# Attention output and its sums regrouped by transfers between partitions instead of by transposes

## The chip, the cores and the metric

The kernel runs on one core of one Trainium2 chip. The core has five engines with a queue of instructions each: TensorE (PE, matmuls and transposes, results in PSUM), VectorE (DVE), ScalarE (ACT), GpSimd (POOL, which does not read PSUM here) and SyncE (SP), which here does nothing but issue DMAs. The metric is device time in microseconds. Before the change two runs took 737.3 and 737.54 us, median 737.42.

## The reference

One PixArt block: batch 16, 256 tokens, width 256, 16 heads of 16, with a condition vector, a self attention, a cross attention to 256 context tokens and an MLP.

```
x_norm = ln(x) * (1 + scale_a) + shift_a
q, k, v = split(x_norm @ W_qkv + b_qkv)                 # 16 heads of 16
attn = softmax(q @ k.T / 4) @ v                         # per head
x = x + gate_a * (attn @ W_proj + b_proj)
q_c = ln(x) @ W_qc + b_qc;  k_c, v_c = split(ln(context) @ W_kvc + b_kvc)
x = x + softmax(q_c @ k_c.T / 4) @ v_c @ W_cproj + b_cproj
h = gelu((ln(x) * (1 + scale_m) + shift_m) @ W_mlp1 + b_mlp1)
x = x + gate_m * (h @ W_mlp2 + b_mlp2)
```

Everything is float32. Products are made of float32r parts: each operand is split into a high part and a low part (what is left), and three products are summed.

## The kernel before

**Units.** Each of the 16 self attentions ("s") and 16 cross attentions ("c") is a unit; the list `seq` (line 786) starts with five s units and then alternates. The loop at line 1219 runs over the units, and each unit has eight steps (`beat`, line 1120). Step k of unit n works on several units at once: it makes the transposed scores and exponentials of two head pairs of unit n (`t_part`, `exp`), the plain scores of unit n+1 and their maxima (`s_tile`; one TensorE product into a bank, one VectorE reduce out of it; two banks, `s0` and `s1`), parts of the Q, K and V projections of later units, and the end of earlier units. After the eight steps of the last unit, the MLP of all samples follows, two matmul stages in four chunks each; its first chunks are interleaved with the end of the last unit in a hand-written order, the string `BE` in `E_` (line 55), whose words are looked up in `done` (line 1232).

**Two lanes.** TensorE's array is used in two halves of 64 rows. `PLAN` (line 1108) gives for every step four strings: words issued before, lane x (rows 0 to 63), lane y (rows 64 to 127), and words issued after. `beside` (line 476) merges the two lanes' instructions by their lengths into TensorE's one queue. "s" and "t" are the scores, a letter with a number is so many matmuls of a projection ("Q12"), "T" and "U" are transposes of a normalised input, "m0" and "m1" of maxima, "E" is the exponential, "o0" and "o1" are the output products. Each half transpose of a tile (`half_turns`, line 342) is four or one pieces of 64 rows; the second half's first piece waits for the first half's last.

**Attention output.** `av_part` (line 769) multiplies exponentials by values. The values tile `vts` (line 86) has 32 columns per head: 16 values and 16 ones, so each head gives 16 rows of output and 16 equal rows of sums; four heads fill 128 rows. Two of these products (one "o" word) fill a bank, which ScalarE copies to the tile oT: [128 rows = 4 heads x 32, 2 groups, 256 tokens]. Each unit has two such tiles, hf = 0 (from "o0") and hf = 1 (from "o1", in the next unit's step 0).

**From there to the projection**, in `build_post` (line 601):

- `pieces` and `halves` (lines 620, 627): four transposes of 128 x 128 per tile, in halves ("A0" in step 6, "A1" in step 2), into psA. Tokens are now rows.
- `norm` (line 630): VectorE takes the reciprocal of 16 sums per row and multiplies, into the tile A ("n0" after step 7, "n1" after step 3).
- `aT` (line 640, made by `transposed`, line 358): four more transposes ("a", step 5) into psT, a ScalarE copy out of PSUM (`evac`, "ae"), and on GpSimd `cut` (line 381, "ac"), a rounded copy (xTh) and a difference (xTl).
- `proj` or lane words "P": 24 half-array matmuls with the projection's weights, in lane x for the unit before and in lane y for the one before that; then `end` ("pe", ScalarE), `add` (GpSimd) and `store`.

**Order.** TensorE, VectorE, ScalarE, GpSimd and SP all keep the order in which the program is written (the class `InOrder`); an engine whose next instruction waits holds up all that stands behind it in its queue. All DMAs of the loop are issued by SP: per unit four transfers for K's high parts, two for K's low part, the same for Q, two small ones for the maxima, a load, and for every second unit a store and a broadcast of gates. The values of K and Q go to a tile `big` in which each head has its rows.

Of the kernel before, what the change touches and what calls it, by code (L numbers as in the profile page):

```python
# [21 lines left out]
def pixart_block(  # L22
# [8 lines left out]
    B, N, H = x.shape  # L31
    NH = 16
    HD = H // NH
    SCALE = HD ** -0.5
    NT = N // P
    KC = H // P
# [18 lines left out]
    E_ = {'CUT': 8, 'LN': {'s': 'pool', 'c': 'pool', 'q': 'pool'}, 'ON': (1, 1, 1), 'L0': -16, 'L1': 1, 'S0': -7, 'A0': 0, 'T0': 1, 'S1': 5, 'A1': 7, 'L2': 9, 'T1': 9, 'S2': 32, 'AP': 23, 'DV': (0, 1), 'HP': (1, 0), 'BZ': {}, 'AV': {1: [(1, 2), (1, 3)], 9: [(0, 0), (0, 1)]}, 'AHEAD': (0, 0, 0, 0, 0, 2), 'TW': {(21, 6): 'cb', (23, 5): 'u0', (23, 7): 'u1', (25, 2): 'u2', (27, 3): 'u3', (27, 7): 'h2a', (28, 0): 'l2 h0p u5', (28, 2): 'h1p', (28, 4): 'h3p', (28, 7): 'u4 u6', (29, 0): 'l3d', (29, 1): 'l0', (29, 2): 'l1', (29, 7): 'h5p', (30, 1): 'u7 h6d h7p', (30, 3): 'h4p', (31, 1): 'l4 l6d', (31, 2): 'l5d x2', (31, 4): 'l7', (31, 7): 'b2'}, 'BE': 'G0 av P g0 A1 G1 G2 N1 F7 g1 S0 PF s2 G3 aT aL p2 a2 G4 x3 b3 S1 S2 T2 C r0 G5 S3 G6 S4 s3 CF x4 F8 g2 G7 S5 F9 p3 S6 G8 a3 r1 G9 F10 G10 T3 g3 b4 S7 s4 F11 S8 S9 F12 G11 p4 a4 F13 r2 S10 G12 x5', 'XP': 1, 'IL': 1, 'MF': 0, 'SH': 4, 'RAMP': 1, 'HA': 1, 'MP': 16, 'W': (7, 1, 0, 0), 'PRE': 'load z0kp silu b12 turn brow L0a z0qp L0b b4 L0d T0t hik scale lok sc1 lg L1a b5 T0h L1b T0l ld2 one0 shift b3 K0a bk hiq lc L1d lp L2a K0m loq K0h T1t K0y0p T1h K0l K0x0 bq hiv K0l0 T1l z1qp K0x1 K0l1 Q0a Q0m K1a K0y1p lov Q0h Q0l Q0x1 K1b Q0l0 bv z1kp V0a Q0l1 Q0x0 Q1a Q1b L2b Q1y0 K1x0 V0b K1l b9 Q0y0p Q0y1p Q1l', 'SL': {(-1, 0): 'L2c ld3 K1l0 K1y1', (-1, 1): 'Q1l0 T2t Q1y1 V1a T2h Q1x0 K1l1 K1x1 T2p', (-1, 2): 'wm V1b Q1x1 z2kp vone', (-1, 3): 'ga K1y0', (-1, 4): 'pb M0 Q1l1 ld4 gs L3a', (-1, 5): 'L3b L3p one1', (-1, 6): 'one2 K2a L3c K2m', (-1, 7): 'z2qp mods cb', (0, 0): 'gm lx sp0', (0, 2): 'sp1 sc2', (0, 3): 'sp3', (0, 6): 'sp2', (1, 4): 'sp4'}}  # L55
# [35 lines left out]
    ones = const.tile([8, N], F32, name="ones")  # L91
# [16 lines left out]
    brow = const.tile([32, P], F32, name="brow")  # L108
# [151 lines left out]
    wm = []  # L260
# [223 lines left out]
    def to_stack(W, src, bias, dst, which, name):  # L484
# [30 lines left out]
        def low_pool():  # L515
            o.lo = work.tile([P, KC, N], F32R, tag="qkl", name=f"l_{name}", bufs=3)
            y = work.tile([P, KC, N], F32, tag="A", name=f"y_{name}", bufs=1)
# [83 lines left out]
    def build_post(u):  # L601
# [18 lines left out]
        def pieces(hf):  # L620
            o.ps = ps_gen(f"psA{hf}_{name}", SHORT)
            return [u.oT[hf][:, r, t * P:(t + 1) * P] for t in range(NT) for r in range(2)]

        def turn(hf):
            whole(pieces(hf), o)

        def halves(hf):
            return half_turns(pieces(hf), o)

        def norm(hf):  # L630
            if hf == 0:
                o.A = work.tile([P, NT, H], F32, tag="A", name=f"A_{name}", bufs=1)
            pv = o.ps.rearrange("p (x h c) -> p x h c", x=4, h=4)
            rc = work.tile([P, 4, 4, 1], F32, tag="rc", name=f"rc{hf}_{name}")
            DVE.reciprocal(rc, pv[:, :, :, HD:HD + 1])
            A = o.A.rearrange("p t (r f) -> p (t r) f", r=2)[:, :, 64 * hf:64 * hf + 64]
            DVE.tensor_tensor(A.rearrange("p x (h i) -> p x h i", h=4),
                              pv[:, :, :, 0:HD], rc.to_broadcast([P, 4, 4, HD]), ALU.mult)

        aT = transposed(lambda: o.A, f"a{name}", pool=True)  # L640

# [38 lines left out]
        o.aT, o.begin, o.gate, o.turn, o.norm, o.proj, o.end, o.add, o.store = aT, begin, gate, turn, norm, proj, end, add, store  # L680
        u.post, o.halves, o.n = o, halves, u.n
# [368 lines left out]
    word["vone"] = lambda: [POOL.memset(v[:, :, :, HD:], 1.0) for v in vts]  # L1050
# [43 lines left out]
    def visit(n, k, home=sp):  # L1094
# [25 lines left out]
    def beat(n, k):  # L1120
# [8 lines left out]
        whole_p = prev and prev.n == nu - 2  # L1129
# [12 lines left out]
        def attention(v, hf):  # L1142
# [12 lines left out]
            "Vk": on(q2 and hasattr(q2, "V"), lambda: q2.V.keep()),  # L1155
# [3 lines left out]
            "ae": on(p1, lambda: p1.aT.evac()), "ac": on(p1, lambda: p1.aT.cut()),  # L1159
            "n1": on(p1, lambda: p1.norm(1)), "n0": lambda: cur.post.norm(0),  # L1160
# [20 lines left out]
            "A1": on(p1, lambda: p1.halves(1)), "A0": lambda: cur.post.halves(0),  # L1181
            "a": on(p1, lambda: p1.aT.halves()),
# [47 lines left out]
    for b in range(2):  # L1230
# [3 lines left out]
        "A1": lambda: o.turn(1), "N1": lambda: o.norm(1), "aT": o.aT.turn, "aL": lambda: (o.aT.high(), o.aT.low_dve()),  # L1234
# [90 lines left out]
```

## Time and profile before

| | |
|---|---|
| median of two runs | 737.42 us |
| profiled execution | 737.4 us, of it 735.6 us span |
| granted TensorE clock | 0.999 |
| busy: PE, DVE, ACT, POOL | 728.9, 584.8, 555.5, 546.3 us |
| DMA packets, bytes | 94825, 90.60 MB |
| attention loop, two units (295.71 to 327.99 us) | 32.28 us |

The span is the time from the first to the last instruction that the profiler saw. Rows of the profile have the form "line engine operation out<-in", and line 51 stands in all of them, since a helper issues every instruction: operations are told apart by their tiles. s is a plain score, st a transposed score, o the output product, psA and psT_a the transposes of the attention output, ps_k, ps_q, ps_v and ps_P the projections, mx the maxima. A trailing s or c names the kind of unit. A time-ordered view has the start in us, the time taken, then the engine and the instruction; SPq is SP's queue. "64*128 64x256" is a matmul of 64 rows by 128 columns of weights with 64 x 256 data, and a "+1 forms" marks that other shapes are in a group. In a bracket stands the idle time before an instruction and what ended it.

### The profile page before, as it was taken

The page shows a single profiled execution, that of the slowest core. Times are in us where ns is not written, and L with a number is a line of the kernel's source. Part 1 is how long each engine was busy: PE and PEld are TensorE (multiplying, and loading weights), DVE is VectorE, ACT ScalarE, POOL GpSimd, SP SyncE. Part 2 cuts the span into 40 slices and gives each one's busy share as a digit, 9 for nine tenths or more (in the row PEclk, how much of TensorE's full clock was granted, in tenths as well). Part 3 has the DMA queues.
Part 4 walks back from the last instruction along what each step waited for, and adds up shares of the span by engine and source line. Part 5 has one row for each costly group of instructions (what it writes and reads, how often), then busy time and mean ns, then how long its engine had stood idle before and what let it go on. Part 6 is the DMA issues. An engine that isn't in the chain of part 4 may idle for free.

```text
span 735.6 us, 25307 instructions
## 1 busy us (share of the span) xinstructions
PE 728.9 (99%) x10112; PEld 644.8 (88%) x10112; DVE 584.8 (79%) x1217; ACT 555.5 (76%) x959; POOL 546.3 (74%) x571
## 2 busy tenths in 40 slices
PE   9999999999999999999999999999999999999997
PEld 9878888888888888888888888888889999999997
DVE  4788898989888888988888989888735577687772
ACT  3268898888888888888888888899887655555553
POOL 6777688869687786968778798788657766767753
PEclk9999999999999999999999999999999999999999
DMA  6754454543545454454545555455312323323331
GB/s 190 205 166 142 125 142 134 141 122 101 155 114 155 125 144 137 107 152 112 160 126 139 143 156 146 126 151 140 96 60 58 102 61 98 98 90 102 87 77 38
DMA packets 94825, 90.60 MB, mean 123 GB/s; under 512 B 9266, under 2 KB 90452, under 8 KB 94708
## 3 DMA queue, kind: packets, MB, share of 16 engines
q1 hardware_dynamic: 94244, 88.20, 42.8%
q8 instruction: 80, 1.31, 0.8%
q0 software_dynamic: 192, 0.52, 0.3%
q14 instruction: 37, 0.30, 0.1%
q10 hardware_dynamic: 272, 0.26, 0.1%
HBM read 26.97 MB, written 8.46 MB: 48 GB/s over the span
## 4 chain that ended last, share of the span: by engine, by line
PE 93%; DVE 3%; POOL 2%; issue 1%; ACT 1%; DMA 1%; SPq 0%; POOLq 0%; ACTq 0%
PE s L51 18%; PE o L51 16%; PE st L51 16%; PE ph L51 10%; PE ps_q L51 5%; PE ps_qc L51 4%; PE ps_v_c L51 3%; PE ps_kc L51 3%; PE ps_P_s L51 3%; PE ps_k L51 2%; PE ps_v_s L51 2%; PE ps_P_c L51 2%; DVE mx L51 1%; PE psT_q L51 1%; PE ps_h L51 1%; PE psA_s L51 1%
## 5 line engine op out<-in xcount | busy, mean ns | idle before, releaser
L51 DVE TENSOR_REDUCE mx<-s 128x2 f32<-128x512 f32 x504 | 324.8, 684 | 64.4 <-PE s L51 57.7
L51 ACT ACTIVATE pt<-st 128x1024 f32<-128x1024 f32 x252 | 258.9, 1027 | 16.4 <-PE st L51 10.4
L51 PE MATMUL s<-big 63*128 63x256 f32 (+1 forms) x1024 | 184.0, 297 | 0.2
L51 PEld LDWEIGHTS s<-big 63*128 63x128 f32 (+1 forms) x1024 | 133.4, 186 | 18.7 <-DVE l_kc L51 6.6
L51 PE MATMUL st<-big 64*128 64x256 f32 (+1 forms) x1024 | 134.6, 298 | 0.5 <-ACT pt L51 0.2
L51 POOL TENSOR_TENSOR hl<-hf,hh 128x512 fp32r<-128x512 f32 x64 | 87.0, 1361 | 52.9 <-ACT hh L51 52.8
L51 PE MATMUL o<-pt,v 128*32 128x256 f32 x2048 | 123.8, 382 | 0.0
L51 PEld LDWEIGHTS st<-big 64*128 64x128 f32 (+1 forms) x1024 | 96.3, 186 | 16.1 <-issue 13.1
L51 PEld LDWEIGHTS o<-pt,v 128*32 128x32 f32 x2048 | 60.1, 110 | 41.4
L51 ACT ACTIVATE hf<-ph,bT 128x256 f32<-128x256 f32 x114 | 47.8, 471 | 33.1 <-PE ph L51 33.0
L51 ACT ACTIVATE hh<-ph,bT 128x256 fp32r<-128x256 f32 x114 | 47.9, 472 | 28.0 <-PE s L51 14.4
L51 ACT COPY oT<-o 128x512 f32<-128x512 f32 x63 | 36.9, 586 | 33.1 <-PE o L51 33.1
L51 PE MATMUL st<-big,hh 128*128 128x256 f32 x256 | 46.7, 282 | 0.0
L51 PE MATMUL s<-big,hh 128*128 128x256 f32 x256 | 46.7, 281 | 0.0
L51 PE MATMUL ph<-wkch,wself 128*128 128x256 f32 x224 | 44.4, 282 | 0.0
L51 PE MATMUL ph<-wqch,wself 128*128 128x256 f32 x224 | 44.3, 282 | 0.0
L51 PE MATMUL ps_k<-xTh_s,wself 64*128 64x256 f32 (+1 forms) x232 | 43.6, 294 | 0.0
L51 POOL TENSOR_SCALAR xn_c<-c,mv_c,rs_c 128x256 f32<-128x256 f32 x32 | 39.0, 1227 | 1.7
L51 PE MATMUL ps_q<-xTh_s,wself 64*128 64x256 f32 (+1 forms) x240 | 39.7, 282 | 0.0
L51 PE MATMUL ps_P_s<-wself,xTh_as 64*128 64x256 f32 x256 | 39.1, 282 | 0.0
L51 PEld LDWEIGHTS s<-big,hh 128*128 128x128 f32 x256 | 39.0, 189 | 0.0
L51 PEld LDWEIGHTS st<-big,hh 128*128 128x128 f32 x256 | 39.0, 189 | 0.0
(250 smaller groups left out, 2500.4 us busy)
## 6 DMA issues: line engine op xcount, KB each, us to landing
big<-h_kc SPq DMA_DIRECT2D x64, 128.0 KB
big<-h_qc SPq DMA_DIRECT2D x64, 128.0 KB
big<-h_k SPq DMA_DIRECT2D x62, 128.0 KB
big<-h_q SPq DMA_DIRECT2D x62, 128.0 KB
big<-l_k SPq DMA_DIRECT2D x32, 128.0 KB
big<-l_q SPq DMA_DIRECT2D x32, 128.0 KB
g<-gd SPq DMA_DIRECT2D x16, 256.0 KB
c<-in_ctx_dram SPq DMA_DIRECT2D x16, 256.0 KB
```

The source lines that it names most:

```text
L51: i = f(*a, **k)
```

## The change

The transposes and the normalisation with tokens as rows go. The values tile now alternates one value and one column of ones, so row 2i of a head's 32 is output i and every odd row is the sum. Per tile two DMAs (`lift`) gather rows by partition stride: the even rows of oT into the tile N (64 rows of 512, which is the layout that the projection needs), and one row of sums per head into the tile S, cut into pieces of 32 (64 rows of 32). When both halves are there, VectorE inverts S in place, 128 x 32 (`recip`). `put` writes it to DRAM, and `get` reads it back so that each head's 512 inverse sums stand in 16 rows (tile R). GpSimd multiplies N by R (`norm`), and `cut` splits the product as before. The step plan is rewritten: the projection of a unit is now in steps 2 to 6 of the unit two later, in both lanes; V's lane x is one unit earlier; the words "d0", "d1" (lift), "rc", "rw", "rr", "ym" take the places shown. Two small tiles of the first steps share the slot of oT; A's slot has two buffers; the third unit's value projection is done before the loop ("V2a V2b").

```diff
-    ones = const.tile([8, N], F32, name="ones")
+    ones = work.tile([8, N], F32, tag="oT", name="ones")
...
-            ACT.copy(vt[:, :, :, 0:HD], o.ps.rearrange("p (t h i) -> p t h i", t=NT, h=NH))
+            ACT.copy(vt[:, :, :, 0:32:2], o.ps.rearrange("p (t h i) -> p t h i", t=NT, h=NH))
...
-        def norm(hf):
...
+        def lift(hf):
+            if hf == 0:
+                o.N = work.tile([P, 2, N], F32, tag="A", name=f"N_{name}", bufs=2)
+                o.S = work.tile([P, 32], F32, tag="rc", name=f"S_{name}")
+            rows = slice(64 * hf, 64 * hf + 64)
+            SP.dma_start(o.S[rows], u.oT[hf][1:128:32].rearrange("h r (j e) -> h (r j) e", e=32))
+            SP.dma_start(o.N[rows].rearrange("p r n -> p (r n)"), u.oT[hf][0:127:2].rearrange("p r n -> p (r n)"))
+
+        def recip():
+            DVE.reciprocal(o.S, o.S)
+
+        def put():
+            o.rd = dram.tile([P, 32], F32, tag="rd", name=f"rd_{name}", bufs=3)
+            SP.dma_start(o.rd, o.S)
+
+        def get():
+            o.R = work.tile([P, 2, N], F32, tag="y", name=f"R_{name}", bufs=2)
+            SP.dma_start(o.R.rearrange("p r n -> p (r n)"),
+                         o.rd.rearrange("(a j) e -> a (j e)", j=16).unsqueeze(1).to_broadcast([8, 16, 512]))
+
+        def norm(eng=POOL):
+            eng.tensor_tensor(o.N, o.N, o.R, ALU.mult)
+            aT.y = o.N
...
     PLAN = [
-        ("kh", "s t m1", "m1 t s", "m1s kH E o1 add gate kl"),
-        ("c1", "s t Q12", "t P2 s P10", "L1 ld kL E"),
-        ("", "s t T pe A1 V3", "s t Q4 T A1 Q1", "hadd E L2 Te Tc c2"),
-        ("", "s t V9", "Q1 t s Q6", "E n1"),
-        ("qh store", "s t", "s t qH", "E L3 o0 ql qL"),
-        ("", "t s a E m0 K6", "t s V4 a m0 V2", "ae ac m0s e5 lc s1"),
-        ("", "s t K1 A0 K5 U E", "V2 t s V4 U A0", "begin e6 Vk Ue s6"),
-        ("", "s t P12", "K2 t s K1 K9", "E n0 Uc s7 e7"),
+        ("", "s t m1", "kh m1 kH s t", "E o1 m1s add gate kl"),
+        ("c1", "s t Q12", "s t V11 d1 V1", "ld E"),
+        ("kL", "L1 s Vk t T P4", "t Q1 s Q3 T", "L2 rc E Te Tc c2"),
+        ("", "s t P8", "Q1 t s Q7", "E rw"),
+        ("e5 qh store", "s t", "s t", "qH E L3 o0 rr ql qL"),
+        ("s1", "t s K1 U m0 K4 E", "t P5 s U m0", "m0s lc e6 Ue Uc"),
+        ("", "K1 s t K6", "s6 P3 t ym s P4", "begin E"),
+        ("", "s t pe V12", "K3 t s K9", "E d0 s7 hadd e7 ac"),
     ]
...
-        on_x = {"Q": (q2, "Q"), "V": (q2, "V"), "K": (q3, "K"), "P": (None if whole_p else p1, None)}
-        on_y = {"Q": (q2, "Q"), "V": (q2, "V"), "K": (q3, "K"), "P": (p2, None)}
+        on_x = {"Q": (q2, "Q"), "V": (q3, "V"), "K": (q3, "K"), "P": (p2, None)}
+        on_y = {"Q": (q2, "Q"), "V": (q2 if n else None, "V"), "K": (q3, "K"), "P": (p2, None)}
...
-        "A1": lambda: o.turn(1), "N1": lambda: o.norm(1), "aT": o.aT.turn, "aL": lambda: (o.aT.high(), o.aT.low_dve()),
+        "A1": lambda: o.lift(1), "N1": lambda: (o.recip(), o.put()), "aT": o.get, "aL": lambda: (o.norm(), o.aT.cut()),
```

At the end of attention the string `BE` is unchanged: "av P g0 A1 G1 G2 N1 F7 g1 S0 PF s2 G3 aT aL p2 a2 G4 x3 b3 S1 S2 T2 C", where p2 and a2 are the power and the product of an MLP layernorm, T2 its transposes on TensorE, and C the last unit's projection.

More of the change, by code (lines that the diff above doesn't have):

```diff
@@ L106, in load_x @@
         SP.dma_start(X[b], tok(x, b))
-    brow = const.tile([32, P], F32, name="brow")
+    brow = work.tile([32, P], F32, tag="oT", name="brow")
     def stage(w_ap, c0, name, tag="pt", bufs=5, t=None, q=SP):
@@ L516, in low_pool @@
             o.lo = work.tile([P, KC, N], F32R, tag="qkl", name=f"l_{name}", bufs=3)
-            y = work.tile([P, KC, N], F32, tag="A", name=f"y_{name}", bufs=1)
+            y = work.tile([P, KC, N], F32, tag="A", name=f"y_{name}", bufs=2)
             for f in range(KC):
@@ L618, in gate @@
             POOL.tensor_tensor(o.xg, X[b], bc_t(G[b][:, 1]), ALU.add)
[L620 to L628, printed above, removed]
-        def norm(hf):
-            if hf == 0:
[L632 to L640, printed above, removed]
+        def lift(hf):
+            if hf == 0:
+                o.N = work.tile([P, 2, N], F32, tag="A", name=f"N_{name}", bufs=2)
[15 more added lines that the diff above has]
+            aT.y = o.N
+        aT = transposed(None, f"a{name}", pool=True)
         def proj(half):
@@ L679, in build_post @@
         o.W, o.src, o.tok, o.name = W, aT, True, f"P_{name}"
-        o.aT, o.begin, o.gate, o.turn, o.norm, o.proj, o.end, o.add, o.store = aT, begin, gate, turn, norm, proj, end, add, store
-        u.post, o.halves, o.n = o, halves, u.n
+        o.lift, o.recip, o.put, o.get = lift, recip, put, get
+        o.aT, o.begin, o.gate, o.norm, o.proj, o.end, o.add, o.store = aT, begin, gate, norm, proj, end, add, store
+        u.post, o.n = o, u.n
     def heads(g):
@@ L1049, in pixart_block @@
         word[f"sp{i}"] = lambda i=i: f_split(i)
-    word["vone"] = lambda: [POOL.memset(v[:, :, :, HD:], 1.0) for v in vts]
+    word["vone"] = lambda: [POOL.memset(v[:, :, :, 1:32:2], 1.0) for v in vts]
     for n, f in (("load", f_load), ("silu", f_silu), ("turn", f_turn), ("brow", f_brow),
@@ L1128, in beat @@
         p1, p2, p3 = (v and v.post for v in map(unit, (n - 1, n - 2, n - 3)))
-        whole_p = prev and prev.n == nu - 2
         if p2 and p2.n > nu - 3:
@@ L1154, in beat @@
             "qH": on(q2 and hasattr(q2, "Q"), lambda: q2.Q.send_high()), "qL": on(q2 and hasattr(q2, "Q"), lambda: q2.Q.send_low()),
-            "Vk": on(q2 and hasattr(q2, "V"), lambda: q2.V.keep()),
+            "Vk": on(n and q2 and hasattr(q2, "V"), lambda: q2.V.keep()),
             "m1s": lambda: m_send(cur, 1), "m0s": on(nxt, lambda: m_send(nxt, 0)),
```

9 lines of the change are left out of this document (4 added, 5 removed).

## The prediction

> **What bounds the kernel now.** I read the page first: the shares of the engines, then the chain that ended last, then the groups. After that came sums over two attention units in mid-kernel, and the time-ordered views of single engines inside them.
>
> ```profile
> PE 728.9 (99%) x10112; PEld 644.8 (88%) x10112; DVE 584.8 (79%) x1217; ACT 555.5 (76%) x959; POOL 546.3 (74%) x571
> PE 93%; DVE 3%; POOL 2%; issue 1%; ACT 1%; DMA 1%; SPq 0%; POOLq 0%; ACTq 0%
> L51 DVE TENSOR_REDUCE mx<-s 128x2 f32<-128x512 f32 x504 | 324.8, 684 | 64.4 <-PE s L51 57.7
> core 0: us, PE busy (x) PEld busy (x) DVE busy (x) ACT busy (x) POOL busy (x), PEclk, DMA share, GB/s
> 295.71:327.99 32.28, 32.27 (x534) 27.41 (x535) 28.05 (x61) 27.24 (x43) 24.54 (x27) 1.00 0.50 138
> ```
>
> TensorE carries 93% of the chain, and VectorE's largest idle time (57.7 us) is spent waiting for score matmuls. So time goes where TensorE's instruction queue goes. The last row is two units (one self, one cross): 32.28 us, 16.14 a unit, at full granted clock. VectorE (14.0 us a unit) and ScalarE (13.6) are not far behind, so a gain on TensorE is capped: VectorE would stop it 2 us further on.
>
> **What is removed on TensorE.**
>
> ```profile
> L51 PE MATMUL psA_s<-ident,oT 64*128 64x64 f32 x256 | 29.3, 227 | 0.0
> L51 PE MATMUL psA_c<-ident,oT 64*128 64x64 f32 (+1 forms) x252 | 27.3, 226 | 0.0
> L51 PE MATMUL psT_as<-ident,A_s 64*128 64x64 f32 x128 | 13.1, 223 | 0.0
> L51 PE MATMUL psT_ac<-ident,A_c 64*128 64x64 f32 (+1 forms) x124 | 13.0, 225 | 0.0
> 300.25 0.22 PE L51 MATMUL psA_s<-ident,oT 64*128 64x64 f32 x1
> 300.29 0.28 PE L51 MATMUL ps_qc<-xTh_q,wqch 64*128 64x256 f32 x1
> 300.31 0.28 PE L51 MATMUL psA_s<-ident,oT 64*128 64x64 f32 x2
> 300.41 0.28 PE L51 MATMUL ps_qc<-xTh_q,wqcl 64*128 64x256 f32 x1
> 300.44 0.22 PE L51 MATMUL psA_s<-ident,oT 64*128 64x64 f32 x1
> ```
>
> All 760 transposes go: 31 units of 24, and 16 more around the last one. Busy times mislead here, since two halves of the array run at once. The starts tell the price: four transposes begin between 300.25 and 300.44, one every 0.062 us, while the other half starts a matmul every 0.12 us. A unit's 24 cost 24 x 0.062 / 2 = 0.74 us of the two-lane stream, as both lanes of the new plan are again of equal length.
>
> **What is removed and added on VectorE and ScalarE.**
>
> ```profile
> L51 DVE TENSOR_TENSOR A_s<-psA_s,rc_s 128x256 f32<-128x256 f32 x32 | 13.6, 425 | 1.1
> L51 DVE RECIPROCAL rc_s<-psA_s 128x16 f32<-128x16 f32 x32 | 8.0, 248 | 0.0
> 302.76 0.66 PE L51 MATMUL s<-big 63*128 63x256 f32 x4
> 315.60 0.42 PE L51 MATMUL s<-big 63*128 63x256 f32 x4
> ```
>
> Per unit VectorE loses 2 x (0.425 + 0.248) = 1.35 us and gains one reciprocal of 128x32 (about 0.25, the price of 128x16); ScalarE loses the copy of the transposed tile out of PSUM. Neither is the bound, but position counts: both old pairs stood between the score reduces of two steps, and the score banks are single. Behind such a pair four score matmuls take 0.66 us, elsewhere 0.42: 0.24 us lost. One of the two places (step 7 to step 0) becomes empty; I credit 0.16 of its 0.24, since the step also has an output product to hide part. At the other place the new reciprocal stands one step earlier, with a wait (below), and I count it even with the old pair.
>
> **What is added on GpSimd.** One 128x512 product a unit.
>
> ```profile
> L51 POOL TENSOR_TENSOR t_s<-t_s,g 128x512 f32<-128x512 f32 x16 | 20.7, 1293 | 0.0
> 317.94 0.61 POOL L51 CAST xTh_c<-y_c 128x512 fp32r<-128x512 f32 x1 [2.66 <-ACT y_c L51]
> 323.78 0.61 POOL L51 CAST xTh_ac<-y_ac 128x512 fp32r<-128x512 f32 x1 [3.86 <-ACT y_ac L51]
> ```
>
> 1.29 us on an engine that has 12.3 us of work in 16.1: 13.6 in about 15.2. It is hidden as long as the 2.7 and 3.9 us of waiting shown above exist. Behind it in GpSimd's order stand the next layernorm products (2.4 us) and the split of the attention output (1.9). The projection that needs that split now comes two steps into the next unit, one unit later than the product it projects, so there is room of about 1 us. I cost it at nothing; without the cover it would be up to 1.29 us a unit.
>
> **What is added on SP's queue.** Six DMAs a unit: two gathers of sums, two of outputs, one to DRAM, one broadcast back. The trace has no such gather, but it has SP's issue times, here for one whole unit:
>
> ```profile
> 312.43 0.55 SPq L51 DMA_DIRECT2D big<-m  x1
> 313.07 2.97 SPq L51 DMA_DIRECT2D big<-h_k  x4
> 316.09 0.59 SPq L51 DMA_DIRECT2D x<-in_x_dram  x1
> 316.78 1.18 SPq L51 DMA_DIRECT2D big<-l_k  x2
> 318.05 0.54 SPq L51 DMA_DIRECT2D x2d<-t_c  x1
> 319.47 2.48 SPq L51 DMA_DIRECT2D big<-h_q  x4
> 322.05 1.20 SPq L51 DMA_DIRECT2D big<-l_q  x2
> 323.89 0.55 SPq L51 DMA_DIRECT2D big<-m  x1
> 324.49 0.39 SPq L51 DMA_DIRECT2D c<-in_ctx_dram  x1
> 324.94 0.46 SPq L51 DMA_DIRECT2D g<-gd  x1
> ```
>
> Eighteen issues take 10.9 us, 0.61 each. Six more at 0.6 make 14.5 of the 15.2 us that I expect of a unit: 95%, in the heavier of the two kinds of unit (the other has 14 issues now: no loads, no store, no gates). Bounds for one new issue are 0.39 (the loads from DRAM) and 0.74 (a quarter of the key sends); I take 0.6, the row of transfers of the same 128 KB. Followed through the new order, nothing waits long: the query sends, behind the put, leave for the broadcast 2.5 us in which the put can land; the low query part, behind the broadcast, lands some 1 us before the score step that reads it. So SP costs nothing, with hardly anything in hand.
>
> **The new wait.** The reciprocal at the end of step 2 waits for a gather issued in step 1, and behind it on VectorE stand the reduces of step 3, whose banks hold up TensorE's scores. How long a transfer takes to land is read off the four-part transpose in the MLP stage:
>
> ```profile
> 605.11 2.58 SPq L51 DMA_DIRECT2D yT<-z  x4
> 609.37 1.74 DVE L51 TENSOR_SCALAR z<-yT,sc,cpT 128x256 f32<-128x256 f32 x2 [1.50 <-DMA yT<-z]
> 627.12 2.49 SPq L51 DMA_DIRECT2D yT<-z  x4
> 632.37 1.41 DVE L51 TENSOR_SCALAR z<-yT,sc,cpT 128x256 f32<-128x256 f32 x2 [2.02 <-DMA yT<-z]
> ```
>
> The last of four parts is issued 1.9 us after the first; its data serve VectorE 2.3 us later (607.1 to 609.4), in the second case 3.4. The gather can issue about 1.6 us after the output product ends (copy 0.6, then the maxima's row, then SP), and lands 3.9 after it; steps 1 and 2 and their reduces take about 3.7. So VectorE waits 0.2 us, at 3.4 us landing 1.3. The first is what I counted even; the second costs up to 1 us a unit.
>
> A rule speaks against this step. The Trainium skill, "DMA: Bandwidth & Descriptors", section "Why a DMA increments its semaphore by 16 and not by 1", says that a DMA spreads over the largest number of engines, up to 16, that divides the slowest dimension of both sides. No row of before separates transfers by this. By it the sums' gather (4 source rows) would use 4 engines and the broadcast (8 rows) 8. As an estimate from it and from the queue's 42.8% of 16 engines over 94,244 packets (53 ns per packet of 0.94 KB), the 256 KB broadcast would need 1.8 us of transfer, not 0.9, and my total would be 0.9 us higher.
>
> ```profile
> q1 hardware_dynamic: 94244, 88.20, 42.8%
> ```
>
> **What only moves.** The values' matmuls go one unit ahead, the projection one unit back, each with its 24 half-array matmuls; the third unit's value matmuls move from the loop into the first steps' stream. The count on TensorE stays, so I cost this at nothing; the cover is that their inputs (the split of the normalised input, three steps earlier; the split output, above) are there. If the split comes late instead, the price is that of GpSimd's missing cover. The values written with stride 2 and the ones between them are the same ScalarE copy and the same one-time fills. The output tiles now come free when a gather has read them and not when TensorE has; two buffers a unit apart leave half a unit for that, against a landing of 2.3 to 3.4 us.
>
> **The end of attention.** The last unit has no next unit to hide its chain.
>
> ```profile
> 553.42 0.69 DVE L51 COPY oT<-o 128x512 f32<-128x512 f32 x1 [3.18 <-PE o L51]
> 559.52 0.72 POOL L51 TENSOR_TENSOR rs_m<-rs_m,mhalf 128x2 f32<-128x2 f32 x1
> 560.27 1.70 DVE L51 TENSOR_SCALAR xn_m<-x,mv_m,rs_m 128x256 f32<-128x256 f32 x2 [0.29 <-POOL rs_m L51]
> 562.02 0.55 PE L51 MATMUL psT_m<-ident,xn_m 128*128 128x128 f32 x3 [0.43 <-DVE xn_m L51]
> ```
>
> On GpSimd the product and the split now stand ahead of the power rs_m of an MLP layernorm, which TensorE needs for its psT_m transposes, in order. From the copy's end at 554.1: gather 2.3, reciprocal 0.25, put 2.3, broadcast 2.3 (561.3), product 1.29, split 0.61 + 1.28, the two small rs_m operations 1.05: 565.7. Before they ended at 560.2. TensorE stands 5.5 us there: what it has queued ahead ends at 561.6 (the psT_m row's start less the 0.43 us that it already waited). With landings of 3.4 us it is 8.8; of 1.7 us, 3.7. Twelve transposes saved there vanish in the wait.
>
> **The sum.** 31 units x (0.74 + 0.16) = 27.9 us less, 5.5 us more: span 735.6 - 22.4 = 713.2. The profiled execution took 737.4, 1.8 outside its span, and the median of the runs is 737.42; so **715 us**. The forecast's own range is 708 (the whole 0.24 saved, 0.1 us of lane switching on top, end at 3.7) to 724 (0.6 us a unit, end at 5.5).
>
> **Rivals.** A measurement of this kernel tells about 2% from no change: 722.7 and 752.2 are the limits.
>
> *The sums arrive late.* Each unit's reciprocal holds VectorE for 1.3 us instead of 0.2, and the reduces and scores behind it move by most of that. For: the gather stands behind four key sends on the same queue. Against: VectorE has an output product right after in which to catch up. With 0.6 to 0.9 of the 0.9 us taken back: span 735.6 - 31 x 0.15 + 5.5 = 736.5, **738 us**, range 724 to 746. In one sentence by itself: the Trainium skill's same page, "Specifications", gives 512 B as the least run for full rate, with read-modify-write below, and the sums travel in runs of 128 B; no run here prices that.
>
> *SP becomes the bound (slower).* If the new issues take what the slow key sends take at worst, or if waits inside SP's order exceed the 0.7 us that the unit leaves, the low query part lands after its score step, and TensorE waits at step 0 of every unit. For: 95% by the sum above; three of the six wait for another engine or for a landing. Against: the lighter units have four issues less, and K and Q are sent a unit ahead. It decides from about 15.3 us of SP time a unit; with 17.0 (six issues at 1.0) the span is 735.6 + 31 x 0.86 + 5.5 = 767.8, **770 us**.
>
> *VectorE was the true cause.* If its 1.1 us less and the even lanes remove the score stalls too, a unit goes to about 14.8 us: 735.6 - 31 x 1.35 + 4 = 697.8, **700 us**. For: VectorE idles on PE, PE on VectorE's banks, in turns. Against: the reduces, 10.3 us a unit, remain.
>
> **Chances.** Forecast 0.52, sums late 0.20, SP bound 0.15, VectorE 0.13. Faster by over 2%: all of the last and nearly all of the forecast, 0.61. Within 2%: the rest and the late sums, 0.24. Slower: 0.15. The range takes in the forecast, nearly all the late sums and most of the VectorE case: 699 to 744.
>
> **What would show it.** Right: no psA and psT_a groups; two units in mid-kernel at 30.3 to 30.8 us; the reciprocal's group with little idle time ended by a DMA; SP with waits of a few tenths; TensorE idle once for about 5 us after the last output product, ended by VectorE's xn_m. Wrong: a wait of the reciprocal of over 1 us a unit, scores waiting for big<-l_q, or GpSimd idle before its new product with the projection waiting for its split.

## The result: 7% slower, and the profile after

The changed kernel took 788.88 us (median of 786.67 and 791.09) against 737.42, a ratio of 1.070, interval 1.057 to 1.083. The forecast was 715 us, at most 744. The profiled execution is the one of 791.09 us, its span 789.3, so 53.7 us have to be found.

First the page of the kernel after: engines, the chain's shares by engine and line, two groups of section 5 (count, busy us, mean ns, idle before and what ended it) and the main DMA queue (packets, MB, share).

```profile
PE 744.8 (94%) x9340; PEld 635.3 (80%) x9340; DVE 557.6 (71%) x1120; ACT 542.5 (69%) x927; POOL 585.1 (74%) x605
PE 67%; DMA 11%; POOL 8%; DVE 5%; issue 4%; ACT 2%; SPq 1%; POOLq 0%; ACTq 0%; DVEq 0%
L51 DVE TENSOR_REDUCE mx<-s 128x2 f32<-128x512 f32 x504 | 326.2, 682 | 125.5 <-PE s L51 120.7
L51 ACT ACTIVATE pt<-st 128x1024 f32<-128x1024 f32 x252 | 258.5, 1026 | 66.7 <-PE st L51 64.5
q1 hardware_dynamic: 112676, 106.04, 48.0%
```

VectorE and ScalarE idle about two and four times as long as in before (64.4 us ahead of the reduces there, 16.4 ahead of the exponentials), while TensorE's share of the chain falls from 93% to 67% and the DMAs' rises from 1% to 11%. So TensorE waits too, and for transfers.

The output products mark the stages: below, the group of tile o in both kernels, first of before, then of after, with count, least, median and greatest ns of one, the first and last start in us, and the commonest form.

```profile
L51 PE MATMUL o<-pt,v x2048: 378/379/404, 45.2 to 552.9; 128*32 128x256 f32 x187
```

```profile
L51 PE MATMUL o<-pt,v x2048: 379/379/634, 45.9 to 594.1; 128*32 128x256 f32 x187
```

The loop between them grew from 507.7 to 548.2 us (40.5 more), what follows it from 182.7 to 195.2 (12.5 more), and 0.7 us came ahead. In the loop the starts of TensorE's matmuls stand more than 0.45 us apart 44 times in after, 42 of them ahead of a plain score, 40.6 us in all; in before twice, and never ahead of a score. One such place in after, first SP's queue and then the chain of waits (start, duration, what):

```profile
405.15 0.54 SPq L51 DMA_DIRECT2D rd_c<-S_c  x1
405.78 0.41 SPq L51 DMA_DIRECT2D x2d<-t_c  x1
406.29 3.83 SPq L51 DMA_DIRECT2D big<-h_q  x4
410.22 0.65 SPq L51 DMA_DIRECT2D R_c<-rd_c  x1
410.96 1.18 SPq L51 DMA_DIRECT2D big<-l_q  x2
```

```profile
411.56 4.40 DMA big<-l_q
416.00 0.50 PE s L51 x3
```

The second low part of the queries is issued at 411.56 right behind the broadcast R, and the score that reads it starts 4.40 us later. The trace's semaphore updates give the landing of every transfer (the last update before the semaphore is used again, counted from the start of the issue). Medians in mid-loop: the low query part lands 2.4 us after its issue in before and 4.0 in after. Counted from the start of output product o0, it lands at 6.41 us in before and at 8.62 in after; in before the next unit's first scores begin at 7.56. Of the 42 pauses, 34 end within 0.4 us of the landing of a low query part, and they make 32.9 of the 40.6 us: that is most of the loss in the loop. The other 8, 7.7 us, end right behind a reduce of the maxima.

### The profile page after: what moved, and what is told of

Read it like the earlier page. It is cut to its first block, busy times and chain, and to the rows that moved or that the text cites. A ratio compares the mean times of both kernels' runs of the same rounds, so it can differ in the third digit from the quotient of the medians.

```text
span 789.3 us, 23993 instructions
## 1 busy us (share of the span) xinstructions
PE 744.8 (94%) x9340; PEld 635.3 (80%) x9340; DVE 557.6 (71%) x1120; ACT 542.5 (69%) x927; POOL 585.1 (74%) x605
## 4 chain that ended last, share of the span: by engine, by line
PE 67%; DMA 11%; POOL 8%; DVE 5%; issue 4%; ACT 2%; SPq 1%; POOLq 0%; ACTq 0%; DVEq 0%
PE s L51 15%; PE st L51 13%; PE o L51 13%; PE ph L51 10%; PE ps_q L51 4%; DVE mx L51 3%; PE ps_qc L51 3%; DMA big<-l_q 3%; DMA big<-l_qc 3%; SPq L51 1%; PE ps_P_s L51 1%; PE ps_kc L51 1%; DMA N_c<-oT 1%; ACT pt L51 1%; POOL xg L51 1%
## 5 line engine op out<-in xcount | busy, mean ns | idle before, releaser
L51 PE MATMUL s<-big 63*128 63x256 f32 (+1 forms) x1024 | 205.3, 313 | 28.3 <-issue 6.9
L51 PEld LDWEIGHTS s<-big 63*128 63x128 f32 (+1 forms) x1024 | 140.0, 185 | 59.9 <-issue 29.1
L51 PE MATMUL st<-big 64*128 64x256 f32 (+1 forms) x1024 | 138.4, 305 | 0.3
L51 PE MATMUL o<-pt,v 128*32 128x256 f32 x2048 | 128.1, 392 | 0.0
L51 POOL TENSOR_TENSOR hl<-hf,hh 128x512 fp32r<-128x512 f32 x64 | 84.5, 1323 | 56.3 <-ACT hh L51 56.1
L51 PEld LDWEIGHTS st<-big 64*128 64x128 f32 (+1 forms) x1024 | 92.4, 186 | 23.8 <-issue 11.9
L51 PE MATMUL ps_P_s<-wself,xTh_as 64*128 64x256 f32 x256 | 43.8, 289 | 0.0
L51 PE MATMUL ps_q<-xTh_s,wself 64*128 64x256 f32 (+1 forms) x240 | 42.6, 285 | 0.0
L51 POOL CAST xTh_q<-y_q 128x512 fp32r<-128x512 f32 x16 | 9.8, 610 | 39.7 <-ACT y_q L51 39.7
```

What stands on the lines that cost most here:

```text
L51: i = f(*a, **k)
```

## Experiments

Two questions are open. For the loss: the theory is that the broadcast of the sums delays the transfers issued behind it, the low query part first; the rivals are SP's issue time and the chain of small transfers by itself. For the gain that is missing: TensorE's stream, as forecast, or another engine's loop, or several loops that are equally tight.

### What in the sums' transfers costs the time

**Taken out, all or one.** Without all transfers of the sums, then without the broadcast alone. In both the division is left out: the outputs are multiplied by themselves.

```diff
-            SP.dma_start(o.S[rows], u.oT[hf][1:128:32]...)   # e3 only, with recip and put
...
-            SP.dma_start(o.R..., o.rd....to_broadcast([8, 16, 512]))
...
-            eng.tensor_tensor(o.N, o.N, o.R, ALU.mult)
+            eng.tensor_tensor(o.N, o.N, o.N, ALU.mult)
```

> Leaves out the sums: no gather of sums, no reciprocal, no put, no broadcast; the outputs are multiplied by themselves in place of by the inverse sums, so that the product on GpSimd stays and waits for nothing. Left of the change: no transposes, the new lanes, the two gathers of outputs. Theories A and B: what is left is the gain that was forecast and no end chain, 703 to 722. Theory C: 760 or more.

> The changed kernel without the broadcast alone: the sums are still gathered, inverted and put to DRAM, and the outputs are multiplied by themselves instead of by the sums (the division is left out). Without any of the sums' transfers it was 746.4 us, with all 788.9. If the broadcast's cost adds to the rest as it did in the kernel before (24.8 us there): 788.9 - 24.8 = 764 us. If the three small transfers and the reciprocal's wait hurt only because the broadcast stands behind them: 746 to 751. If the broadcast is not the larger part here: over 770.

Measured: 746.41 us without all (ratio 1.0127, 1.0091 to 1.0163), 753.24 without the broadcast (1.0208, 1.0187 to 1.0228). So 35.6 of the 51.5 us hang on the broadcast and on the product's wait for it, which is gone as well; by the marks of the profiled executions, 31.9 us less in the loop than in after and 5.7 in the tail. Another 6.8 hang on the two gathers, the reciprocal and the put. The remaining 9.0 are there with no sums at all: by the marks of the loop, its span of 745.8 us has 7.5 more than before's in the tail and 2.8 more in the loop. In that tail TensorE still stands 5.1 us ahead of psT_m (the row below: total us, times, longest), so the product and the split ahead of the power on GpSimd cost time there without any wait for sums. Without the broadcast the low query part lands at 6.22 us again.

```profile
PE psT_m L51 <- DVE xn_m L51: 6.1, 3, 5.1
```

**The broadcast alone, in the kernel before.** One transfer a unit is added to before, into a tile that nobody reads (x7; two small tiles of the first steps share the slot of oT, as in the change); then the same bytes from 16 rows (x10).

```diff
+            SP.dma_start(R, gd[0:8, 0:2].rearrange("b a h -> b (a h)").unsqueeze(1).to_broadcast([8, 16, 512]))
...
-        ("qh store", "s t", "s t qH", "E L3 o0 ql qL"),
+        ("qh store", "s t", "s t qH", "E L3 o0 rr ql qL"),
```

> The kernel before with one transfer a unit added: a broadcast of 8 rows of 2 KB to 128 partitions (256 KB, from DRAM that is there anyway, into a tile nobody reads), issued ahead of the low query part, where the changed kernel has it; nothing else is changed. Theory: the broadcast alone moves the low query part's landing from 3.1 us to about 5 us behind its issue, so that it lands just when its score step comes: SP has time left here, so it takes a part of the changed kernel's loss, +5 to +20 us (742 to 757). Rival (the issue slots of all six new DMAs together do it, the broadcast's own traffic does nothing): no change, within 4 us.

> The kernel before with the added broadcast, as in the run that gave 761.8 us, but read from 16 rows of DRAM instead of 8 (16 rows, 8 times each; the same 256 KB, one issue): by the number of semaphore updates it is spread over 16 engines instead of 8. Theory: what hurts is the time for which the broadcast's pieces fill the queues of the engines that it is on, ahead of the low query part: with half as many pieces on each engine about half of the 24.8 us comes back, 747 to 756. Rival (only the bytes count, or the issue slot): the same 761.8, within 4 us.

Measured: 761.77 us against 737.0 (1.033, 1.0284 to 1.0376), and 750.91 against 737.25 (1.0185, 1.0146 to 1.0223). No wait on data was added, no other engine has more to do, and yet 24.8 us go. Spread over 16 rows it is 13.7: 11.1 come back. The broadcast posts 9 semaphore updates from 8 rows and 16 from 16 rows; it lands 4.6 and 4.0 us after its issue, the low query part behind it 4.1 and 3.7. So the number of rows, and with it of updates, is about half of the cost. The low query part's own 16 updates show the sharing. In mid-loop of before hardly one comes later than 3.0 us after the issue; behind the broadcast from 8 rows it is in most cases 8 of them, in x7 as in after, while the other 8 come nearly as early as in before (in x7 2.2 to 2.7 and 3.5 to 4.1 us, in before 2.1 to 2.4). Which engine an update is from, the trace does not say. The issue slot counts too: in x7 the low query part is issued 0.5 us later after o0. How the rest splits between slot and bytes, these runs do not separate.

**The order of the two transfers, the rows, the queue.** In the changed kernel: the broadcast behind the low query part (e1); sums written twice and read from 16 rows (e2); put and get issued by ScalarE instead of SP (e6).

```diff
-        ("e5 qh store", "s t", "s t", "qH E L3 o0 rr ql qL"),
+        ("e5 qh store", "s t", "s t", "qH E L3 o0 ql qL rr"),     # e1
...
-            SP.dma_start(o.R..., o.rd.rearrange("(a j) e -> a (j e)", j=16).unsqueeze(1).to_broadcast([8, 16, 512]))
+            SP.dma_start(o.R..., o.rd.rearrange("a d f -> (a d) f").unsqueeze(1).to_broadcast([16, 8, 512]))   # e2
+            ACT.dma_start(o.R..., ...)                            # e6, put too
```

> One edit of the changed kernel: in step 4 the two sends of Q's low part go to SP's queue before the broadcast of the inverse sums, not behind it. Theory A (the low query part lands too late for the next unit's first score step, because the broadcast stands ahead of it and fills part of the DMA engines): its landing comes 2.3 us earlier (0.75 of issue, 1.6 of transfer), the attention loop loses most of its 1.3 us a unit against before, total 735 to 755. Theory B (SP has simply too many issues): the same number of issues, only 0.75 us of them out of the way, total 765 to 780. Theory C (the new order of the lanes itself costs the time): no change, 780 to 790.

> The order stays; the inverse sums are written twice to DRAM, so that the broadcast has 16 source rows in place of 8, at the price of one more small issue on SP. Theory A with the spread over DMA engines as its cause: the broadcast lands in about 3.2 us in place of 4.5, the low query part behind it 1 us earlier, total 760 to 775. Theory B: one issue more, 788 to 800. If the number of source rows does not matter: 786 to 795.

> The changed kernel with the put and the broadcast of the sums issued by ScalarE's DMA queue in place of SP's, at the same places of the program. Theory A (the low query part and the maxima stand behind the broadcast in SP's queue): SP has 1.2 us less to issue a unit and its transfers share engines with the broadcast but do not stand behind it: low query part 1.5 us earlier, the loop near 16.3 us a unit, total 752 to 765. If only the bytes on the engines matter and not the place in the queue: 775 to 790. If ScalarE's 1.2 us of issue is what the exponentials lack: over 790.

Measured: 802.5 us (1.0869, 1.081 to 1.0929), 785.49 (1.0639, 1.0603 to 1.0675) and 774.76 (1.0523, 1.0498 to 1.0549). The first is worse than the change itself. TensorE's waits of e1 (total us, times, longest) say why:

```profile
PE st L51 <- DMA big<-m: 26.5, 23, 3.1
```

The low query part lands at 6.37 us as in before, but now the maxima m stand behind the broadcast and land at 8.76 instead of 6.02. Whatever is issued next pays. In e6 SP issues the low query part as early as before (2.75 us after o0, before 2.70), but it lands at 7.91: a queue of its own does not take the broadcast out of the way. The Trainium skill, "DMA: Bandwidth & Descriptors", section "Issuing engines are not separate DMA queues", says that DMAs of all issuing engines run on the same 16 DMA engines and interleave, so that a second issuer saves issue time only; the trace agrees, with 0.8 us of issue won (after: 3.57) and a landing still 4.3 us behind the issue. In e2 the low query part lands 3.4 us after its issue in place of 4.0, but with one more put in the queue it is issued 0.7 us later after o0 than in after; the gain of 3.4 us is little beyond the spread of its runs (783.2 to 787.1).

**The tail, and all mendings together.** The last unit's product stands later in the tail's order (e4); then e2, e4 and e6 in one kernel (e7).

```diff
-s2 G3 aT aL p2 a2 G4 x3 b3 S1 S2 T2 C r0 G5 S3 G6 S4 s3
+s2 G3 aT p2 a2 G4 aL x3 b3 S1 S2 T2 r0 G5 S3 G6 S4 C s3
```

> Only the order at the end of attention changes: the last unit's product and split on GpSimd go behind the power of the MLP layernorm and one difference of the hidden layer, and its projection goes four MLP pieces later. If the end costs its 12 us because the power and the transposes that need it stand behind the wait for the broadcast: 776 to 781, with the loop as it was. If the end costs them for another reason: 786 to 791.

> The changed kernel with three of the mendings together: sums put to DRAM and broadcast back on ScalarE's DMA queue, the broadcast read from 16 rows (one more put), and the last unit's product later in the tail. Singly they gave 14.1, 3.4 and 4.8 us. If they are separate losses: 788.9 - 22.3 = 766.6 us. If the first two mend the same wait: about 770. A floor is the kernel without any transfer of the sums, 746.

Measured: 784.04 us (1.0633, 1.0595 to 1.067) and 772.25 (1.0468, 1.0447 to 1.049). Together they give 16.6 us, less than the sum of 22.3. No version that still has the sums comes near before.

### Why the removed transposes gain nothing

**One engine relieved at a time.** In the kernel before: without the 24 half transposes, so that tokens and features stay in the wrong places (x2), with each reduce over half of the keys (x3), both (x4), with half of each exponential (x5), that without transposes (x6), with the low parts of the splits left out (x11). x3 takes the maxima of half of the keys.

```diff
-            return half_turns(pieces(hf), o)
+            return iter(()), iter(())                                        # x2, x4, x6; norm reads oT
...
-            DVE.tensor_reduce(..., side(home, bank).rearrange("p (j n) -> p j n", j=2), ...)
+            DVE.tensor_reduce(..., side(home, bank).rearrange("p (j n) -> p j n", j=2)[:, :, :P], ...)   # x3, x4
...
-        ACT.activation(u.pt[pair]..., st..., AF.Exp, scale=SCALE)
+        ACT.activation(u.pt[pair][:, 0]..., st[:, 0], AF.Exp, scale=SCALE)   # x5, x6
...
-            POOL.tensor_tensor(lo, o.y, hi, ALU.subtract)                    # x11; the high part is used twice
```

> The kernel before without the 24 half transposes a unit and nothing else: VectorE's reciprocal and product read the output tile, ScalarE's copy reads the product, all from SBUF in place of PSUM, so that tokens and features stand in the wrong places. No new DMA and the old lanes. Theory D (TensorE's instruction stream is the bound, each transpose has its price of 0.03 us of two-lane time): 31 x 0.74 less, 712 to 718. Theory E (a unit's length is set by the score banks going to and fro between TensorE, VectorE and ScalarE, and the transposes only fill its gaps): 731 to 737.

> The kernel before with each score reduce taking the maximum of 128 of its 256 columns (the maxima are those of half the keys): VectorE's largest operation goes from 0.65 to about 0.38 us, TensorE's work stays whole. Theory D: no change, 734 to 737. Theory E: the banks come free earlier and the units shorten by 0.3 us or more, 720 to 728.

> Both edits of the last two kernels, no transposes and half reduces. Theory D: as without the transposes, 712 to 718. Theory E: only now do the transposes show their price, 700 to 712.

> The kernel before, with each exponential taken over one of its two banks only (128x512 instead of 128x1024, about 0.59 us instead of 1.03), and the output products reading that half for both; half of the exponentials are left out. Theory F (a unit is set by the loop between TensorE and ScalarE through the one tile of transposed scores: four matmuls, exponential, next four matmuls; the transposes only fill that wait): the loop loses 0.44 us in each of its eight steps, 3.5 us a unit, and the unit falls from 16.1 us until TensorE's own pace stops it, by the starts about 14.4 us (per unit 160 half-array matmuls at 0.115/2, 64 output matmuls at 0.06, 41 half transposes at 0.062/2): 685 to 700 us. The forecast's theory (TensorE's stream is the bound): nothing, 737. Score banks and VectorE: nothing, 737.

> The same, and the 24 half transposes of a unit are left out as well (their results are read from the tiles in SBUF instead). Alone, leaving them out gave 1.0037. Theory F: with the loop out of the way TensorE's pace decides, and now the 24 count with 0.062/2 us each, 0.74 us a unit: 15 to 23 us below the kernel with half exponentials. If another loop holds the unit: the same as that kernel, within 5 us.

> The kernel before with only GpSimd relieved: the low parts of the splits are left out (1.28 us for each split), everything else is as before, the transposes too. Four reliefs together gave 706, three without this one 733. Theory G (several loops equally tight): alone it gains little, 730 to 737 us. If GpSimd's chain was the single bound of the kernel before: most of the 31 us, 706 to 715.

Measured: 739.7 us (ratio 1.0037), 735.23 (0.9966), 741.49 (1.0049), 734.66 (0.9961), 735.53 (0.998), 738.56 (1.0017). None of the intervals lies further than 0.7% from no change. Every theory that names one engine as the bound fell: TensorE's stream, VectorE's score banks, ScalarE's exponentials, GpSimd's splits. Where a gain goes is seen in the waits of TensorE's weight loads between 150 and 450 us, first of before, then of x2:

```profile
PEld st L51 <- issue: 7.4, 18, 0.4
PEld s L51 <- DVE l_kc L51: 4.1, 10, 0.4
PEld s L51 <- DVE l_k L51: 3.7, 9, 0.4
PEld s L51 <- DVE mx L51: 0.2, 1, 0.2
```

```profile
PEld st L51 <- issue: 7.4, 18, 0.4
PEld s L51 <- DVE mx L51: 6.3, 23, 0.5
PEld st L51 <- ACT pt L51: 4.2, 19, 0.3
PEld s L51 <- DVE l_kc L51: 4.1, 10, 0.4
PEld s L51 <- DVE l_k L51: 3.7, 9, 0.4
PEld ps_P_s L51 <- POOL xTl_as L51: 2.1, 9, 0.3
```

New are 6.1 us for the reduces, 4.2 for the exponentials and 2.1 for GpSimd's split: 12.4 us in the 18.6 units of this window, 0.67 us a unit. That is nearly the 0.74 us that the transposes took. They had filled time in which three other engines were still at work.

**Several at once.** Transposes out, half reduces and half exponentials (x8); the splits shortened too (x9); the same as x9, but the transposes kept (x12). The edits are those above.

> The kernel before without the half transposes, with half of each exponential and half of each score reduce (maxima over half of the keys, exponentials of half of the scores left out): TensorE, VectorE and ScalarE all relieved at once. Theory G (no single bound: TensorE's stream, VectorE's score banks, ScalarE's exponentials and GpSimd's split ahead of the projection each have a loop within a few tenths of 16 us, so that what one gives back another takes): GpSimd's split still holds every second unit at 16.4 to 16.7 us, as without transposes and with half reduces, the other units fall to about 15: 715 to 735 us. If all three were the whole of it: 13.7 to 14.4 us a unit, 665 to 690. If something else entirely holds 16 us (the low query part's transfer): 737.

> The same, and GpSimd relieved too: the low parts of the split transposed inputs and of the split attention output are left out (the high part is used in their place), 1.28 us for each split. Theory G: now the units fall together, to 14 to 15 us: 675 to 705 us. If the chain of the low query part (output product, sends, landing, next score step) holds 16 us: as the run with three relieved, near 735, with TensorE's waits before the scores of step 0.

> Half reduces, half exponentials and short splits together, but with the half transposes and their normalisation and copies as in the kernel before; beside the run with all four reliefs (706.3 us) this prices the transposes where VectorE, ScalarE and GpSimd have room. Forecast's price, 0.74 us a unit of TensorE's stream: 706 + 23 = 729 us. If the transposes are worth nothing to TensorE even then: 706 to 710.

Measured: 733.3 us (0.9937, 0.9908 to 0.9966), 706.31 (0.9576, 0.9554 to 0.9597) and 722.13 (0.9781, 0.9759 to 0.9802). TensorE's longest wait in x8 between 100 and 480 us (total, times, longest):

```profile
PE ps_P_s L51 <- POOL xTh_as L51: 14.9, 12, 1.6
```

With three engines relieved, the fourth holds every second unit: GpSimd's split of the attention output. (The granted clock of this execution is 0.980; what part that has was not tried.) With all four relieved 31 us are gained, though each alone moved the time by no more than 2.4, up or down. GpSimd's relief was not run with one other alone, so whether all four are needed is not shown. And now the transposes have a price: x12 less x9 is 15.8 us, 0.51 a unit (in x12 the normalisation also reads PSUM as in before, in x9 SBUF). The marks of the loop agree, first in x12, then in x9:

```profile
L51 PE MATMUL o<-pt,v x2048: 379/379/631, 44.2 to 538.6; 128*32 128x256 f32 x187
```

```profile
L51 PE MATMUL o<-pt,v x2048: 379/379/634, 44.0 to 522.2; 128*32 128x256 f32 x187
```

494.4 against 478.2 us. What holds x9 at 15.0 us a unit stays open.

## Why the prediction was wrong, point by point

**"These 24 cost 0.74 us of the two-lane stream" (what is removed on TensorE).** This step failed. Where the price shows at all it is 0.51 us a unit (x12 against x9), two thirds of the forecast's, and the forecast credited it to the unit as if TensorE were the bound; alone it is worth nothing (x2). The busy share of 99% misled: without the transposes, x2's page still has 98%, with 756 matmuls fewer; the profile's legend says that the ends of matmuls are modelled. Only the weight loads' share moves, from 88% to 85%:

```profile
PE 724.0 (98%) x9356; PEld 623.9 (85%) x9356; DVE 606.4 (82%) x1217; ACT 553.2 (75%) x959; POOL 550.8 (75%) x571
```

The trace of before had the warning. Its paces, start to start, are 0.12 us for a half-array matmul, 1.86 for the 32 of an output product and 0.062 for a half transpose. A unit in mid-kernel has 160 half-array matmuls, two output products and 40 half transposes: 160/2 x 0.12 + 2 x 1.86 + 40/2 x 0.062 make 14.6 us of the 16.1. The other 1.5, an estimate from these paces, were waits that do not show as idle TensorE. The Trainium skill, "Perfetto Trace Analysis", section "Identifying the Most-Contended Engine", calls matmul busy time no good measure of how close TensorE is to its limit and points, among others, to the busy share of the weight loads; these runs agree, with 99% and 98% for the matmuls and 88% and 85% for the loads.

**The empty place on VectorE, 0.16 us a unit.** Failed for the same reason. In x3 the reduces, of which this was a matter, take half as long, and 2.1 us come of it in all.

**The product on GpSimd, hidden.** Its size was right (1.27 us; forecast 1.29). In after GpSimd also waits for the broadcast ahead of it (rows under the reciprocal, below). What that costs was not tried by itself.

**SP costs nothing; the low query part lands 1 us before its score.** This is the step that failed most. The issue times were as forecast (0.58 for a gather, 0.53 for the outputs, 0.65 for the broadcast), and SP's issuing took 77% of the time between 150 and 450 us, against 61% before. But the landing was taken as fixed. It depends on what was issued just ahead: 2.4 us alone, 4.0 behind the broadcast. The forecast weighed the broadcast's place in SP's queue and its own landing, and not that the transfer behind it shares its DMA engines. Taking the broadcast out of the changed kernel gives 35.6 us, putting it into the kernel before costs 24.8 (e8, x7). Part of the difference is the tail, where in the changed kernel the product waits for the broadcast: e8 gains 5.7 us there, x7 loses 0.1. In the loop it is 31.9 against 20.5 us in the profiled executions; why, where SP is fuller, stays open.

**The reciprocal's wait, 0.2 us.** Held in 28 of 32 units, where it did not wait at all. VectorE's and GpSimd's waits for the sums over the whole span (total us, times, longest), then the reciprocal with one of its long waits:

```profile
DVE S_c L51 <- DMA S_c<-oT: 12.7, 3, 4.9
```

```profile
POOL N_s L51 <- DMA R_s<-rd_s: 13.3, 10, 2.6
POOL N_c L51 <- DMA R_c<-rd_c: 12.2, 10, 3.2
```

```profile
550.72 0.35 DVE L51 RECIPROCAL S_c<-S_c 128x32 f32<-128x32 f32 x1 [3.43 <-DMA S_c<-oT]
```

The reciprocal waited three times in the 16 c units (3.4, 4.9 and, in the tail, 4.4 us) and once in the s units (1.2 us). What it gathers at 550.7 was copied by 544.2, but SP issued the gather at 548.87 only, behind an MLP weight load and four key sends. The reduces behind it came late, and TensorE stood ahead of their scores, 3.7 us from start to start; behind the wait of 1.2 us it was 1.5.

**The spread over engines.** The rule of the Trainium skill, "DMA: Bandwidth & Descriptors", section "Why a DMA increments its semaphore by 16 and not by 1", held in count: the sums' gather (4 rows) has 5 updates, the broadcast (8 rows) 9, the maxima (2 rows) 3, and the transfers with 16 rows or more 16. That is one for each engine and one more where they are fewer than 16; the section says that the issuing sequencer adds the rest at once, and the trace agrees: the first of the broadcast's 9 updates comes 1.1 us after the issue, the others from 3.6 us on (medians). The sentence that priced it at 0.9 us of one landing was far too low, because it looked at the broadcast and not at the one behind it. With 16 rows 11.1 of 24.8 us came back (x10).

**What only moves, nothing.** Not contradicted: without the sums the loop is 2.8 us longer than before's, all gains and losses of the new order together.

**The end, 5.5 us.** The place was right, the size was not. (The terms of that sum add to 565.5, not 565.7.) The chain of the tail in after:

```profile
596.49 3.14 DMA S_c<-oT
599.71 0.36 DVE S_c L51
600.09 1.42 DMA rd_c<-S_c
601.53 5.13 DMA R_c<-rd_c
606.79 1.25 POOL N_c L51
608.11 0.62 POOL xTh_ac L51
608.80 1.26 POOL xTl_ac L51
```

The broadcast took 5.13 us instead of 2.3, and the gather 3.14 behind 1.2 us in which SP had two other transfers to issue; the put was shorter, 1.42. TensorE stood 7.29 us ahead of its psT_m transposes (row below). The tail as a whole lost 12.5 us; a smaller pause, 2.0 us from start to start, lies ahead of the last projections. Since 5.1 of the 7.29 us remain without any sums (e3), the chain of transfers is the smaller part of this wait, and the product and split on GpSimd the larger. Moving them in the order (e4) brought 4.8 us; in the profiled executions the tail is 6.5 us shorter and the loop 2.7 longer.

```profile
612.70 0.45 PE L51 MATMUL psT_m<-ident,xn_m 128*128 128x128 f32 x1 [7.29 <-DVE xn_m L51]
```

**The rivals.** "SP becomes the bound" named the right symptom, scores that wait for big<-l_q, and the right side. Its cause, SP's issuing, is the smaller part: with put and get off SP (e6) 14.1 us come back, without the broadcast 35.6. "The sums arrive late" happened in the few units above and not in each; "VectorE was the true cause" did not happen.

## What to carry to other kernels

Before crediting a removed instruction to an engine at 99%, add up the paces of its starts: where they fill 90% of the period, the rest is waits, and what is removed turns into longer waits unless the other engines' loops are shortened too (one relief gave nothing, four together 31 us). A new transfer is priced by what is issued behind it: a broadcast of 256 KB that nobody read cost 24.8 us, because the transfer that the next scores need stood next in line. Gathering by DMA to save cheap transposes, on a queue whose transfers are all due within a microsecond or two, is paid at that place, and changing the order only changes who pays.

## What was not expected of the hardware

The landing of 128 KB goes from 2.4 to 4.0 us behind a 256 KB broadcast on 8 engines and to 3.7 behind one on 16, and with ScalarE as the issuing engine it is 4.3. And TensorE's granted clock falls to half after some short pauses. Windows of after (from:to in us, length, busy us of PE, PEld, DVE, ACT and POOL with counts, granted clock, DMA share, GB/s):

```profile
410.00:415.00 5.00, 3.79 (x53) 3.26 (x49) 2.93 (x7) 3.90 (x7) 2.84 (x4) 1.00 0.73 188
415.00:420.00 5.00, 4.35 (x42) 2.24 (x42) 2.73 (x6) 1.02 (x1) 4.66 (x5) 0.66 0.88 238
...
605.00:610.00 5.00, 0.41 (x4) 0.20 (x2) 0.00 (x0) 0.00 (x0) 3.07 (x3) 0.78 0.14 44
610.00:615.00 5.00, 1.56 (x6) 1.30 (x7) 2.78 (x3) 0.00 (x0) 3.50 (x5) 0.50 0.00 0
615.00:620.00 5.00, 5.00 (x33) 5.00 (x32) 2.92 (x7) 3.83 (x8) 1.94 (x2) 0.70 0.00 0
620.00:625.00 5.00, 5.00 (x45) 5.00 (x44) 3.75 (x8) 2.67 (x7) 3.61 (x5) 1.00 0.33 108
```

After the pause from 413.5 to 415.55, 2.04 us from start to start, the next window has 0.66, and the long pause of the tail leads to 0.50 and 0.70; over the whole span the clock is 0.984 against 0.999. In the loop it stood at 0.50 three times, for 3.41 us each, from 416.64, 488.32 and 553.18 us, behind pauses of 2.04, 1.80 and 3.07 us; a pause of 2.37 us that ended at 380.24 was not followed by it. The Trainium skill, "TensorE: Matmul & The Clock Gate", section "Part 1: The HAM clock gate", gives half rate after an idle window of about 3.4 us; the pause at 413.5 was shorter than that and was followed by half the clock all the same. What the lost clock costs here was not measured by itself; an estimate of its most in the loop is half of the three times 3.41 us, 5.1 us.
